# A macaron transformer block in float32: a separate buffer for the softmax sums, one for the attention's transposed tokens, and another order of blocks

## The chip, the core and the metric

The kernel runs on one core of a Trainium2 chip. The metric is the time of one execution on the device in microseconds (us). Each kernel is run several times and the median is compared. The profile is of one further execution.

The engines are called PE (TensorE, matrix products), DVE (VectorE), ACT (ScalarE), POOL (GpSimd) and SP (SyncE, which here only issues DMAs). "PEld" is the loading of a matmul's stationary operand.

## The reference

Eight sequences of 512 tokens with 512 features each go through a half feed-forward network, an attention and another half feed-forward network. Everything is float32.

```python
x = x + 0.5 * ffn(layernorm(x))      # the first half
x = x + attention(layernorm(x))
x = x + 0.5 * ffn(layernorm(x))      # the second half

# ffn: width 2048; of every four neighbours only the two largest are kept
h = silu(x @ w_gate) * (x @ w_up)
h = keep_two_of_four(abs(h)) * h
y = h @ w_down

# attention: 16 heads of 32, 4 key/value heads, rotary positions
scores = einsum('bhqd,bhkd->bhqk', rope(q), rope(k)) / 32 ** 0.5
out = einsum('bhqk,bhkd->bhqd', softmax(scores), v) @ W_o
```

## The kernel before

**Two kinds of work.** The feed-forward work is done in 16 *blocks*, one for each sequence b and each half: (b, 0) is the half before the attention, (b, 1) the one after. A block is a generator (`ffn`) that emits matmuls in *groups*. Its gate and up products (`woven`) are arranged in seven products of quarter matrices instead of eight (a Strassen-like scheme): each `product` is four matmuls of 128x128 by 256 columns, and is called with a PSUM bank named x, v or z. Its down products (y, `products`) are eight such matmuls each. A block has `WIDTH` = 42 groups, and a product of gate and up counts half a group.

Everything else runs *beside* the blocks as *sides*: the layernorm of the next block (`layernorm_t`) and the attention of a sequence (`attention`). A side is a generator too. Between two groups of the block in hand the main loop may let a side take one step, which emits a few instructions. So TensorE's order, a single queue, is: product, product, a step of attention, product, and so on. The work of a side fits where the waits of its operands have passed while TensorE worked on products.

**What decides when a side steps.** The builder keeps its own clock of three engines (`at["pe"]`, `at["dve"]`, `at["act"]`), which it moves on as it emits instructions (`takes`, `multiplied`). Each side has a first and a last group between which its steps are paced, with a weight for each step (`WEIGHTS`). A side steps when its turn has come (`due`) and when what it yielded as *ready* lies before TensorE's time on that clock. If it is `LATE` = 3 groups overdue, it steps regardless. VectorE's work is held in three queues (`urgent`, `put_off`, `for_later`, through `soon` and `later`), from which `fill` takes what fits beside TensorE; `ensure` emits what is asked for at once. All of this only fixes the order of instructions. On the chip, semaphores decide when they run.

**The attention of one sequence.** After its layernorm and the projections of k, q and v, it goes through four quarters of heads c = 0 to 3 (four heads at a time on 32-row tiles of TensorE), and in each through four row tiles t = 0 to 3:

- `scores(c + 1, t)`: four matmuls into sc, four reductions on DVE for the row maxima nm. The maxima are split into three bf16 pieces z (`in_pieces`), transposed by TensorE (tr) and copied by ACT into mT (`pieces_by_row`).
- `exponentials(c, t)`: the transposed scores st, with the maxima subtracted by four small matmuls, then one exponential on ACT from st into p, four heads by 512 at once.
- `weighted`: four matmuls from p into the output ops.
- `summed`: DVE adds the previous p onto this one, in place: p(t) += p(t-1), four adds for each t > 0. As the add changes p(t), it comes after the matmuls `weighted` have read p(t). The buffers for p are two (`p_slots`), used in turn.
- `divided`: after t = 3, four matmuls with ones sum p over rows into den; ACT takes its reciprocal by Ln and Exp (two changes of the function table); DVE multiplies ops by it into qT. It is emitted right behind the next quarter's first st.

There is one PSUM slot of four banks for sc and st, one bank for ops, and three banks for all else (`Bank`).

The attention's own layernormed, transposed tokens xT are in the pool `xtp` with two buffers, which the feed-forward blocks' xT share; the list `in_xT` counts who holds one, and a layernorm's transposes wait until one is free.

**Order of the blocks.** (0,0), (1,0), (2,0), (0,1), (3,0), (1,1), (4,0), (2,1), (5,0), (3,1), (6,0), (4,1), (7,0), (5,1), (6,1), (7,1). An attention begins at the earliest 16 groups after the end of its first half, and must be done 13 groups before its second half; they follow each other. By the formulas in the code they get 55, 59, 72, 72, 65, 58.8, 69.1 and 55 groups, with 7 to 19 groups without an attention in four places.

Of the kernel before, what the change touches and what calls it, by code (L numbers as in the profile page):

```python
# [11 lines left out]
FP = mybir.dt.float32  # L12
# [14 lines left out]
def macaron_block(  # L27
# [59 lines left out]

    Q11, Q12, Q22, Q21, S1, S2, S3, S4 = range(8)
    gu_sums = [dram.tile([P, 4, 2, ND // 2, P], FP, name=f"gu_{i}") for i in range(2 * NCH)]
    blocks = [(0, 0), (1, 0)]  # L90
    for b in range(2, B):
        blocks += [(b, 0), (b - 2, 1)]
    blocks += [(B - 2, 1), (B - 1, 1)]
    coming = deque()
    for block in blocks:
        for i in range(2 * NCH):
# [61 lines left out]
    class Later:  # L158
# [8 lines left out]
        def fits(self, slack):  # L167
            return max(at["dve"], self.ready) + self.us <= at["pe"] + slack

    def later(us, does, ready=None, queue=put_off):  # L170
        queue.append(Later(us, does, pe_heard() if ready is None else ready, queue))
        return queue[-1]
# [42 lines left out]
    class Bank:  # L215
        def __init__(self, shape, name, dtype=FP):
            self.slot = min(banks, key=lambda slot: max(slot[2], when(slot[1]), at["pe"]))
            banks.remove(self.slot)
            takes("pe", 0.0, max(self.slot[2], ensure(self.slot[1])) + TOLD)
            self.slot[1:] = [], 0.0  # L220
            self.tile = ps_mm.tile(shape, dtype, tag=f"mm{self.slot[0]}", name=name)

# [39 lines left out]
    def by_scalar():  # L262

        return at["act"] - BEHIND
# [3 lines left out]
    def layernorm_t(got, tag, src=None, xb=None):  # L268
# [33 lines left out]

        def turn(t):
            if t == 0:
                assert len(in_xT) < 2
                in_xT.append(got)
                got["xT"] = xtp.tile([P, ND, S], FP, tag="xT", name="xT")
            xT = got["xT"]
            tr = transposed([xn[t][:, c * P : (c + 1) * P] for c in range(ND)])
            nc.scalar.copy(xT[:, :, t * P : (t + 1) * P], tr.tile)  # L310
            tr.free(end=takes("act", 0.6, pe_heard()))
# [11 lines left out]
        if xb is None:  # L323
            there = at["pe"] + 10.0
            yield lambda: there
            found = [soon(0.9, partial(moments, t)) for t in (0, 1)]
            yield now
            found += [soon(0.9, partial(moments, t)) for t in (2, 3)]
            yield partial(when, found[:2])
            ensure(found[:2])  # L330
            scales((0, 1))
            yield partial(when, found)
            ensure(found)
            scales((2, 3))
            yield by_scalar
            for t in range(NT):
                normalise(t)
                end = at["act"]
                yield by_scalar if t < NT - 1 else lambda: max(end, by_scalar()) if len(in_xT) < 2 else None
            for t in range(NT):  # L340
                turn(t)
                yield by_scalar if t < NT - 1 else now
            if tag == "xf":
                sums()
        else:

            function(AF.Sqrt)
            for t in range(NT + 1):
                if t < NT:
                    moments(t)  # L350
                    va = rs[:, 0, t : t + 1]
                    nc.vector.tensor_scalar(va, mv[:, t, 1:2], EPS, None, ALU.add)
                    nc.scalar.activation(va, va, AF.Sqrt)
                if t:
                    i = t - 1
                    nc.vector.reciprocal(rs[:, 1, i : i + 1], rs[:, 0, i : i + 1])
                    nc.vector.tensor_scalar(
                        xn[i], xb[:, i, :], mv[:, i, 0:1], rs[:, 1, i : i + 1], ALU.subtract, ALU.mult
                    )
                    turn(i)  # L360
            function(AF.Silu)
            sums()
# [149 lines left out]
    def ffn(b, final, last):  # L512
# [90 lines left out]
        def woven(h, i, r, last_one):  # L603
# [4 lines left out]

            def product(bank, q, rhs, first, ready=0.0):
                lhs = quarters[(b, final), i, q]  # L610
                takes("pe", 0.0, ready + TOLD)
                for m in range(2):
                    for k in range(2):
                        nc.tensor.matmul(  # L614
# [23 lines left out]
            product(x, Q11, b11, True)  # L638
            end = copied(left, x.tile)
            yield 0.5  # L640
            takes("pe", 0.0, ensure(normed[b, final].pop("made", ())) + TOLD)
            v = Bank([P, 2, HALF], "v")
            product(v, S1, ts[:, 0], True, ensure(gu_made.pop(i, ())))
            at_corner = copied(corner, v.tile)
# [117 lines left out]
    def attention(b):  # L762
# [15 lines left out]
        def projected(dst, col, scale):  # L778
# [13 lines left out]
            ps.free([read])  # L792
            soon(0.65, partial(nc.vector.scalar_tensor_tensor, sw, sw, scale, cs[:, 1, :], ALU.mult, ALU.mult))
            made = soon(0.65, partial(nc.vector.tensor_tensor, dst, dst, sw, ALU.add))
            return [p_slots.used(w_slots.used(made))]

        of_k = projected(kT, D, 1.0)
        yield now
# [14 lines left out]
                )  # L813
        multiplied(3.57)
        fill()
        in_xT.remove(got)
        nc.scalar.copy(v, vps.tile)
        vps.free(end=takes("act", 0.6, pe_heard()))
        wo = wa_slots.tile([P, ND, D + 2 * KV], FP, "wo")
# [3 lines left out]
        def scores(c, t, nm):  # L823

            sc = sc_slots.tile([P, N_KV, S], FP, "sc")
            for kv, rows in enumerate(heads):
                nc.tensor.matmul(  # L827
                    out=sc[:, kv, :], lhsT=qT[rows, c, t * P : (t + 1) * P], rhs=kT[rows, :], start=True, stop=True
                )
# [22 lines left out]
            tr.free(end=takes("act", 0.6, pe_heard()))  # L852
            return mT

        def exponentials(c, t, mT):

            st = sc_slots.tile([P, N_KV, S], FP, "st")
            p = p_slots.tile([P, N_KV, S], FP, "p")
            for kv, rows in enumerate(heads):
                nc.tensor.matmul(  # L860
                    out=st[:, kv, :], lhsT=kT[rows, t * P : (t + 1) * P], rhs=qT[rows, c, :], start=True, stop=False
# [4 lines left out]
            multiplied(1.29, True)  # L866
            function(AF.Exp)
            nc.scalar.activation(p, st, AF.Exp)  # L868
            end = takes("act", 1.88, max(pe_heard(), p_slots.ready + 0.1))
            return p, end  # L870

        def weighted(t, ops, p):

# [3 lines left out]
                )  # L877
            multiplied(1.0, True)

        def summed(p, before):  # L880

            if before is None:
                return []
            for kv in range(N_KV):
                made = later(0.6, partial(nc.vector.tensor_tensor, p[:, kv], p[:, kv], before[:, kv], ALU.add))
            return [p_slots.used(p_slots.used(made), 1)]

        def divided(c, ops, p, sums):

            ensure(sums)  # L890
            den = Bank([P, S], "den")
            for kv, rows in enumerate(heads):
                nc.tensor.matmul(out=den.tile[rows, :], lhsT=ones32, rhs=p[:, kv, :], start=True, stop=True)  # L893
            multiplied(1.0, True)
            rT = w_slots.tile([P, S], FP, "rT")
            function(AF.Ln)
# [16 lines left out]
            yield partial(when, found)  # L913
        pieces = in_pieces(nm)
        yield partial(when, pieces)
        p = before = last = None
        out_of = []
        for c in range(ND):
            ensure(pieces)
            mT = pieces_by_row()  # L920
            turned = at["act"]
            nm = maxima()
            for t in range(NT):


                if t == 1:
                    ops = acc_slots.tile([P, S], FP, "ops")
                if p is not None:
                    weighted((t - 1) % NT, ops, p)
                if c + 1 < ND:  # L930
                    found = scores(c + 1, t, nm)
                if p is not None:
                    sums = summed(p, before)
                    before = p if t else None
                    if t == 0:
                        last = (c - 1, ops, p, sums)
                if c + 1 < ND:
                    yield partial(lambda f, turned: max(when(f), turned), found, turned)
                p, end = exponentials(c, t, mT)
                there = []  # L940
                if t == 0 and last is not None:
                    there = out_of = divided(*last)
                elif t == NT - 1 and c + 1 < ND:
                    there = pieces = in_pieces(nm)
                yield partial(lambda there, end: max(when(there), end), there, end)
        weighted(NT - 1, ops, p)
        last = (c, ops, p, summed(p, before))
        yield partial(when, last[3])
        xts = []
        for t in range(NT):  # L950
            xts.append(xnp.tile([P, D], FP, tag="xa", name="xt"))
            nc.sync.dma_start(out=xts[t], in_=tokens[b][1][t * P : (t + 1) * P, :])
        out_of = divided(*last)
        yield partial(when, out_of)
        ensure(out_of)
        for t, xt in enumerate(xts):
            y = Bank([P, D], "y")
            for k in range(ND):
# [21 lines left out]
    NORM = 5 + 2 * NT  # L980

    WEIGHTS = [0.5] * (NORM + ND + 2) + [0.7] * (NT + 1) + [0.9, 0.9] * NT
    WEIGHTS += ([0.9, 1.5] + [0.9, 0.9] * (NT - 1)) * (ND - 2) + [1.5] + [1.3] * (NT - 1) + [0.9] * 2 + [0.5] * NT
    ATTENTION = len(WEIGHTS)

    def place(b, i):
# [4 lines left out]
    for b, i in blocks[1:]:  # L991
        stage = partial(layernorm_t, normed[b, i], "xf", tokens[b][2 * i])
        sides.append((place(b, i) - 15, place(b, i) - 2, NORM, stage, ("attention", b) if i else None, None))
    before = 0
    for b in range(B):

        left = place(B - 1, 1) - 13 - before
        first = max(before, place(b, 0) + WIDTH + 16)
        if first % WIDTH > 17:
            first += WIDTH - first % WIDTH  # L1000
        last = min(place(b, 1) - 13, max(before + left / (B - b), first + 1.4 * WIDTH))
        assert last - first > ATTENTION * 0.8
        sides.append((first, last, ATTENTION, partial(attention, b), ("attention", b - 1) if b else None, ("attention", b)))
        before = last
    sides.sort(key=lambda s: s[0])

    for _ in layernorm_t(normed[0, 0], "xf", xb=xs[0, 0]):
# [98 lines left out]
```

## Time and profile before

| | before |
|---|---|
| median of 3 runs | 3256.96 us (3256.67 to 3257.97) |
| profiled execution, its own time | 3256.3 us |
| its span, first to last instruction | 3254.5 us |
| TensorE clock granted | 0.998 of full speed |
| DMA queue of all tensors, share of 16 engines' time | 42.6% |
| last matmul ends | 4.0 us before the end of the span |

How to read the profile's rows. A *group* row gives source line, engine, operation, output and inputs by name, shapes, the count, then busy time in us and mean ns of one, then the engine's idle time before them and what ended it. A float32 matmul is recorded as two. The matmuls of the tiled stretches (sc, st, ops, den) run four at a time, so the mean of one says little; busy time divided by the number of groups is the figure to use. A *wait* row gives the waiting engine, tile and line, whom it waited for, and then the total in us, the number of waits and the longest. A *timeline* row gives start and duration in us, engine, line, operation and count, and in brackets the idle time before it. Line 164 is the helper that runs DVE's queued work (L164), so its rows are told apart by the tile.

### The profile page before, as it was taken

What the parts mean: (1) busy time and instruction counts of PE and PEld (TensorE: products, weight loads), DVE (VectorE), ACT (ScalarE), POOL (GpSimd) and SP (SyncE); (2) the same over time, 40 slices, a digit from 0 to 9 for tenths busy, and PEclk for the clock granted to TensorE, in tenths of its full rate; (3) what the DMA queues carried; (4) which work ended last, traced back from release to release, by engine and by line L of the source; (5) the groups of instructions that cost most, each with busy time, mean ns of one, the idle gap of its engine ahead of it and who ended that gap; (6) DMA issues with size and microseconds to landing.
All of it is one profiled execution on the core that took longest, in us unless ns stands there. A gap on an engine that the chain in (4) does not pass through costs nothing.

```text
span 3254.5 us, 43735 instructions
## 1 busy us (share of the span) xinstructions
PE 3207.1 (99%) x15880; PEld 2322.9 (71%) x15880; DVE 2274.8 (70%) x4894; ACT 1194.5 (37%) x1680; POOL 603.3 (19%) x888
## 2 busy tenths in 40 slices
PE   8999999999999999999999999999999999999999
PEld 6886668766776667776776668666776678666786
DVE  6867865677677775876678866687577765787554
ACT  2222452145324441354314532146324542255221
POOL 2422002210220112111221112111120122100220
PEclk9999999999999999999999999999999999999999
DMA  6762335433533434444443345333533446234451
GB/s 229 246 218 96 111 126 174 144 120 107 191 111 123 156 114 161 134 129 140 163 147 122 121 148 195 117 117 111 198 99 117 156 128 209 95 109 139 151 174 46
DMA packets 249285, 463.21 MB, mean 142 GB/s; under 512 B 24432, under 2 KB 64368, under 8 KB 248304
## 3 DMA queue, kind: packets, MB, share of 16 engines
q1 hardware_dynamic: 249072, 460.42, 42.6%
q8 instruction: 127, 2.08, 0.3%
q14 instruction: 86, 0.70, 0.1%
HBM read 421.53 MB, written 38.80 MB: 141 GB/s over the span
## 4 chain that ended last, share of the span: by engine, by line
PE 93%; DVE 3%; DMA 1%; ACT 1%; issue 1%; POOL 0%; SPq 0%; DVEq 0%; ACTq 0%; POOLq 0%
PE x L614 25%; PE y L542 23%; PE v L614 12%; PE z L614 6%; PE proj L782 4%; PE sc L827 4%; PE ops L875 4%; PE st L860 4%; PE y L959 3%; PE den L893 2%; PE tr L252 2%; PE gu L589 1%; DVE p L164 1%; PE vps L807 1%; PE y L572 1%; PE st L865 1%
## 5 line engine op out<-in xcount | busy, mean ns | idle before, releaser
L614 PE MATMUL x<-ts,w 128*128 128x256 f32 x3000 | 721.9, 384 | 9.5 <-DVE corner L628 6.4
L614 PEld LDWEIGHTS x<-ts,w 128*128 128x128 f32 x3000 | 560.9, 191 | 157.6 <-issue 55.0
L542 PE MATMUL y<-wd,h 128*128 128x256 f32 x1984 | 451.3, 382 | 6.4 <-ACT rT L897 2.9
L542 PEld LDWEIGHTS y<-wd,h 128*128 128x128 f32 x1984 | 372.4, 190 | 93.1 <-issue 27.5
L436 POOL TENSOR_TENSOR e<-h 128x512 f32<-128x512 f32 x62 | 99.1, 1598 | 1625.2 <-DVE h L430 1504.5
L868 ACT ACTIVATE p<-st 128x2048 f32<-128x2048 f32 x128 | 239.6, 1872 | 392.6 <-DVE p L164 199.6
L164 DVE TENSOR_REDUCE nm<-sc 128x1 f32<-128x512 f32 x512 | 322.2, 683 | 60.7 <-PE sc L827 58.6
L542 PE MATMUL y<-wd,e 128*128 128x256 f32 x1488 | 336.5, 381 | 1.2 <-DMA wd<-wd 1.2
L555 DVE SCALAR_TENSOR_TENSOR x<-y,x 128x512 f32<-128x512 f32 x372 | 242.3, 685 | 131.8 <-PE y L542 129.9
L542 PEld LDWEIGHTS y<-wd,e 128*128 128x128 f32 x1488 | 280.0, 190 | 58.6 <-issue 16.5
L244 ACT ACT_TABLE_LOAD x224 | 287.4, 1283 | 4.7 <-PEq L1095 0.7
L164 DVE TENSOR_TENSOR p<-p 128x512 f32<-128x512 f32 x384 | 256.4, 724 | 32.3 <-PE ops L875 32.3
L232 ACT COPY row<-x 128x512 f32<-128x512 f32 x194 | 113.5, 585 | 404.8 <-PE x L614 403.9
L663 ACT ACTIVATE h<-x 128x256 f32<-128x256 f32 x125 | 47.5, 380 | 576.2 <-PE x L614 544.1
L614 PE MATMUL x<-xT,w 128*128 128x256 f32 x1000 | 240.8, 384 | 0.0
L614 PE MATMUL z<-xT,w 128*128 128x256 f32 x1000 | 239.4, 382 | 0.0
L614 PE MATMUL v<-xT,w 128*128 128x256 f32 x1000 | 238.9, 382 | 0.2
L614 PE MATMUL v<-ts,w 128*128 128x256 f32 x1000 | 238.4, 381 | 0.4 <-DVE ts L164 0.3
L614 PEld LDWEIGHTS x<-xT,w 128*128 128x128 f32 x1000 | 186.7, 191 | 53.7 <-issue 23.4
L614 PEld LDWEIGHTS z<-xT,w 128*128 128x128 f32 x1000 | 186.4, 190 | 49.4 <-issue 22.8
L614 PEld LDWEIGHTS v<-xT,w 128*128 128x128 f32 x1000 | 187.4, 190 | 46.2 <-issue 10.9
L614 PEld LDWEIGHTS v<-ts,w 128*128 128x128 f32 x1000 | 187.6, 190 | 40.4 <-issue 9.1
(106 smaller groups left out, 4067.7 us busy)
## 6 DMA issues: line engine op xcount, KB each, us to landing
w<-gu SPq DMA_DIRECT2D x472, 256.0 KB, 3.3
w<-in_w_gu SPq DMA_DIRECT2D x394, 256.0 KB, 3.3
wd<-wd SPq DMA_DIRECT2D x155, 512.0 KB, 4.0
wd<-in_w_down SPq DMA_DIRECT2D x124, 256.0 KB, 4.9
x<-x SPq DMA_DIRECT2D x64, 256.0 KB, 2.6
xn<-x SPq DMA_DIRECT2D x64, 256.0 KB, 6.8
x<-in_x SPq DMA_DIRECT2D x32, 256.0 KB, 3.3
gu<-w SPq DMA_DIRECT2D x32, 256.0 KB, 2.6
```

The costliest lines, as they stand in the source:

```text
L164: self.does()
L232: nc.scalar.copy(dst, src)
L244: nc.scalar.activation(dummy[:, 1:2], dummy[:, 0:1], f)
L436: nc.gpsimd.tensor_tensor(sums[:, 2], h11, h12, ALU.add)
L542: nc.tensor.matmul(out=y.tile[:, t, :], lhsT=part[:, t * P : (t + 1) * P], rhs=operands[i][:, n, :], start=(n == 0), stop=(n == 3),)
L555: nc.vector.scalar_tensor_tensor(to, y.tile, 0.5 * sign, to, ALU.mult, ALU.add)
L614: nc.tensor.matmul(out=bank.tile[:, m, :], lhsT=lhs[:, m, k, :], rhs=rhs[:, k, :], start=(first and m == 0 and k == 0), stop=(k == 1), ski ...
L782: nc.tensor.matmul(out=ps.tile, lhsT=wa[:, k, col : col + P], rhs=xT[:, k, :], start=(k == 0), stop=(k == ND - 1))
L827: nc.tensor.matmul(out=sc[:, kv, :], lhsT=qT[rows, c, t * P : (t + 1) * P], rhs=kT[rows, :], start=True, stop=True)
L860: nc.tensor.matmul(out=st[:, kv, :], lhsT=kT[rows, t * P : (t + 1) * P], rhs=qT[rows, c, :], start=True, stop=False)
L868: nc.scalar.activation(p, st, AF.Exp)
L875: nc.tensor.matmul(out=ops[rows, :], lhsT=v[:, t, rows], rhs=p[:, kv, :], start=(t == 0), stop=(t == NT - 1))
```

## The change

1. **Sum of exponentials in a buffer of its own.** In each quarter the exponential at t = 0 goes into `total`, those at t = 1, 2, 3 into `other`, one and the same buffer. DVE adds `other` onto `total` (`added`), from the end of the exponential on. `divided` takes den from `total`, and is emitted after the next scores and before the next st. For the last quarter it is emitted right after the last `weighted`, without a step between.
2. **The attention's transposed tokens** take a slot of `p_slots` instead of a buffer of `xtp`. So rope tables (cs), transposed tokens, `total` and `other` use the two slots in turn. Only the blocks' own xT are counted in `in_xT`.
3. **Order of blocks**: (0,0), (1,0), (2,0), (3,0), (0,1), (4,0), (1,1), (2,1), (5,0), (6,0), (3,1), (7,0), (4,1), (5,1), (6,1), (7,1). Every attention gets the same number of groups, (617 - 58) / 8 = 69.9, one right after the other.
4. **The builder's clock** is told of more waits (`waits`): for the slot of sc and st until its exponential is done, for ops, for p, for the pieces, for the sums. Steps yield more of what they need as their readiness. Two weights of the steps become others (1.5 to 1.2, and two of 0.9 to one of 1.5, as there is one step less).

```diff
-    blocks = [(0, 0), (1, 0)]
-    for b in range(2, B):
-        blocks += [(b, 0), (b - 2, 1)]
-    blocks += [(B - 2, 1), (B - 1, 1)]
+    first_of = {0: 0, 1: 1, 2: 2, 3: 3, 5: 4, 8: 5, 9: 6, 11: 7}
+    second_of = {4: 0, 6: 1, 7: 2, 10: 3, 12: 4, 13: 5, 14: 6, 15: 7}
+    blocks = [(first_of[i], 0) if i in first_of else (second_of[i], 1) for i in range(2 * B)]
...
+    class Done:
+        def __init__(self, end):
+            self.end = end
+    def waits(end):
+        takes("pe", 0.0, end + TOLD)
...
             if t == 0:
-                assert len(in_xT) < 2
-                in_xT.append(got)
-                got["xT"] = xtp.tile([P, ND, S], FP, tag="xT", name="xT")
+                if tag == "xf":
+                    assert len(in_xT) < 2
+                    in_xT.append(got)
+                    got["xT"] = xtp.tile([P, ND, S], FP, tag="xT", name="xT")
+                else:
+                    got["xT"] = p_slots.tile([P, ND, S], FP, "xT")
...
-        def exponentials(c, t, mT):
+        def exponentials(c, t, mT, p, free):
             st = sc_slots.tile([P, N_KV, S], FP, "st")
-            p = p_slots.tile([P, N_KV, S], FP, "p")
+            waits(sc_slots.ready)
...
-            end = takes("act", 1.88, max(pe_heard(), p_slots.ready + 0.1))
-            return p, end
+            end = takes("act", 1.88, max(pe_heard(), free + 0.1))
+            sc_slots.used(Done(end))
+            return end
...
-        def summed(p, before):
-            if before is None:
-                return []
+        def added(p, end):
             for kv in range(N_KV):
-                made = later(0.6, partial(nc.vector.tensor_tensor, p[:, kv], p[:, kv], before[:, kv], ALU.add))
-            return [p_slots.used(p_slots.used(made), 1)]
+                made = later(0.6, partial(nc.vector.tensor_tensor, total[:, kv], total[:, kv], p[:, kv], ALU.add), end + HEARD)
+            return [made]
-        def divided(c, ops, p, sums):
-            ensure(sums)
+        def divided(c, ops, sums):
+            waits(ensure(sums))
...
+        total = p_slots.tile([P, N_KV, S], FP, "total")
+        other = p_slots.tile([P, N_KV, S], FP, "p")
...
                 if c + 1 < ND:
                     found = scores(c + 1, t, nm)
-                if p is not None:
-                    sums = summed(p, before)
-                    before = p if t else None
-                    if t == 0:
-                        last = (c - 1, ops, p, sums)
+                out_of = []
+                if t == 0 and c > 0:
+                    out_of = divided(c - 1, ops, sums)
                 if c + 1 < ND:
-                    yield partial(lambda f, turned: max(when(f), turned), found, turned)
-                p, end = exponentials(c, t, mT)
-                there = []
-                if t == 0 and last is not None:
-                    there = out_of = divided(*last)
-                elif t == NT - 1 and c + 1 < ND:
-                    there = pieces = in_pieces(nm)
-                yield partial(lambda there, end: max(when(there), end), there, end)
+                    yield partial(when, there + found)
+                p = other if t else total
+                end = exponentials(c, t, mT, p, ensure(sums))
+                sums = added(p, end) if t else []
+                if t == NT - 1:
+                    out_of += sums
+                    if c + 1 < ND:
+                        pieces = in_pieces(nm)
+                        out_of += pieces
+                yield partial(when, [Done(end)] + out_of)
+        waits(end)
         weighted(NT - 1, ops, p)
-        last = (c, ops, p, summed(p, before))
-        yield partial(when, last[3])
+        out_of = divided(c, ops, sums)
...
-    before = 0
-    for b in range(B):
-        left = place(B - 1, 1) - 13 - before
-        first = max(before, place(b, 0) + WIDTH + 16)
-        if first % WIDTH > 17:
-            first += WIDTH - first % WIDTH
-        last = min(place(b, 1) - 13, max(before + left / (B - b), first + 1.4 * WIDTH))
+    bounds = [WIDTH + 16 + b * (place(B - 1, 1) - 13 - WIDTH - 16) / B for b in range(B + 1)]
+    for b, (first, last) in enumerate(zip(bounds, bounds[1:])):
         sides.append((first, last, ATTENTION, partial(attention, b), ("attention", b - 1) if b else None, ("attention", b)))
-        before = last
```

More of the change, by code (lines that the diff above doesn't have):

```diff
@@ L89, in macaron_block @@
     gu_sums = [dram.tile([P, 4, 2, ND // 2, P], FP, name=f"gu_{i}") for i in range(2 * NCH)]
-    blocks = [(0, 0), (1, 0)]
-    for b in range(2, B):
-        blocks += [(b, 0), (b - 2, 1)]
-    blocks += [(B - 2, 1), (B - 1, 1)]
+    first_of = {0: 0, 1: 1, 2: 2, 3: 3, 5: 4, 8: 5, 9: 6, 11: 7}
+    second_of = {4: 0, 6: 1, 7: 2, 10: 3, 12: 4, 13: 5, 14: 6, 15: 7}
+    assert B == 8
+    blocks = [(first_of[i], 0) if i in first_of else (second_of[i], 1) for i in range(2 * B)]
     coming = deque()
@@ L218, in __init__ @@
             banks.remove(self.slot)
-            takes("pe", 0.0, max(self.slot[2], ensure(self.slot[1])) + TOLD)
+            waits(max(self.slot[2], ensure(self.slot[1])))
             self.slot[1:] = [], 0.0
@@ L338, in layernorm_t @@
                 end = at["act"]
-                yield by_scalar if t < NT - 1 else lambda: max(end, by_scalar()) if len(in_xT) < 2 else None
+                yield by_scalar if t < NT - 1 else (
+                    lambda: max(end, by_scalar()) if tag == "xa" or len(in_xT) < 2 else None
+                )
             for t in range(NT):
@@ L610, in product @@
                 lhs = quarters[(b, final), i, q]
-                takes("pe", 0.0, ready + TOLD)
+                waits(ready)
                 for m in range(2):
@@ L640, in woven @@
             yield 0.5
-            takes("pe", 0.0, ensure(normed[b, final].pop("made", ())) + TOLD)
+            waits(ensure(normed[b, final].pop("made", ())))
             v = Bank([P, 2, HALF], "v")
@@ L794, in projected @@
             made = soon(0.65, partial(nc.vector.tensor_tensor, dst, dst, sw, ALU.add))
-            return [p_slots.used(w_slots.used(made))]
+            return [p_slots.used(w_slots.used(made), 1)]
         of_k = projected(kT, D, 1.0)
@@ L815, in attention @@
         fill()
-        in_xT.remove(got)
         nc.scalar.copy(v, vps.tile)
@@ L853, in pieces_by_row @@
             return mT
-        def exponentials(c, t, mT):
+        def exponentials(c, t, mT, p, free):
             st = sc_slots.tile([P, N_KV, S], FP, "st")
-            p = p_slots.tile([P, N_KV, S], FP, "p")
+            waits(sc_slots.ready)
             for kv, rows in enumerate(heads):
@@ L878, in weighted @@
             multiplied(1.0, True)
-        def summed(p, before):
-            if before is None:
-                return []
+        def added(p, end):
             for kv in range(N_KV):
-                made = later(0.6, partial(nc.vector.tensor_tensor, p[:, kv], p[:, kv], before[:, kv], ALU.add))
-            return [p_slots.used(p_slots.used(made), 1)]
-        def divided(c, ops, p, sums):
-            ensure(sums)
+                made = later(0.6, partial(nc.vector.tensor_tensor, total[:, kv], total[:, kv], p[:, kv], ALU.add), end + HEARD)
+            return [made]
+        def divided(c, ops, sums):
+            waits(ensure(sums))
             den = Bank([P, S], "den")
             for kv, rows in enumerate(heads):
-                nc.tensor.matmul(out=den.tile[rows, :], lhsT=ones32, rhs=p[:, kv, :], start=True, stop=True)
+                nc.tensor.matmul(out=den.tile[rows, :], lhsT=ones32, rhs=total[:, kv, :], start=True, stop=True)
             multiplied(1.0, True)
@@ L915, in attention @@
         yield partial(when, pieces)
-        p = before = last = None
-        out_of = []
+        total = p_slots.tile([P, N_KV, S], FP, "total")
+        other = p_slots.tile([P, N_KV, S], FP, "p")
+        p, sums = None, []
         for c in range(ND):
-            ensure(pieces)
+            waits(ensure(pieces))
             mT = pieces_by_row()
-            turned = at["act"]
+            there = [Done(at["act"])]
             nm = maxima()
             for t in range(NT):
-                if t == 1:
-                    ops = acc_slots.tile([P, S], FP, "ops")
                 if p is not None:
+                    if t == 1:
+                        ops = acc_slots.tile([P, S], FP, "ops")
+                        waits(acc_slots.ready)
+                    waits(end)
                     weighted((t - 1) % NT, ops, p)
@@ L931, in attention @@
                     found = scores(c + 1, t, nm)
-                if p is not None:
-                    sums = summed(p, before)
-                    before = p if t else None
-                    if t == 0:
-                        last = (c - 1, ops, p, sums)
-                if c + 1 < ND:
-                    yield partial(lambda f, turned: max(when(f), turned), found, turned)
-                p, end = exponentials(c, t, mT)
-                there = []
-                if t == 0 and last is not None:
-                    there = out_of = divided(*last)
-                elif t == NT - 1 and c + 1 < ND:
-                    there = pieces = in_pieces(nm)
-                yield partial(lambda there, end: max(when(there), end), there, end)
+                out_of = []
+                if t == 0 and c > 0:
+                    out_of = divided(c - 1, ops, sums)
+                if c + 1 < ND:
+                    yield partial(when, there + found)
[8 more added lines that the diff above has]
+                yield partial(when, [Done(end)] + out_of)
+        waits(end)
         weighted(NT - 1, ops, p)
-        last = (c, ops, p, summed(p, before))
-        yield partial(when, last[3])
+        out_of = divided(c, ops, sums)
         xts = []
@@ L952, in attention @@
             nc.sync.dma_start(out=xts[t], in_=tokens[b][1][t * P : (t + 1) * P, :])
-        out_of = divided(*last)
         yield partial(when, out_of)
-        ensure(out_of)
+        waits(ensure(out_of))
         for t, xt in enumerate(xts):
@@ L982, in macaron_block @@
     WEIGHTS = [0.5] * (NORM + ND + 2) + [0.7] * (NT + 1) + [0.9, 0.9] * NT
-    WEIGHTS += ([0.9, 1.5] + [0.9, 0.9] * (NT - 1)) * (ND - 2) + [1.5] + [1.3] * (NT - 1) + [0.9] * 2 + [0.5] * NT
+    WEIGHTS += ([0.9, 1.2] + [0.9, 0.9] * (NT - 1)) * (ND - 2) + [1.5] + [1.3] * (NT - 1) + [1.5] + [0.5] * NT
     ATTENTION = len(WEIGHTS)
@@ L993, in macaron_block @@
         sides.append((place(b, i) - 15, place(b, i) - 2, NORM, stage, ("attention", b) if i else None, None))
-    before = 0
-    for b in range(B):
-        left = place(B - 1, 1) - 13 - before
-        first = max(before, place(b, 0) + WIDTH + 16)
-        if first % WIDTH > 17:
-            first += WIDTH - first % WIDTH
-        last = min(place(b, 1) - 13, max(before + left / (B - b), first + 1.4 * WIDTH))
-        assert last - first > ATTENTION * 0.8
+    bounds = [WIDTH + 16 + b * (place(B - 1, 1) - 13 - WIDTH - 16) / B for b in range(B + 1)]
+    for b, (first, last) in enumerate(zip(bounds, bounds[1:])):
+        assert place(b, 0) + WIDTH + 16 <= first and last <= place(b, 1) - 13
         sides.append((first, last, ATTENTION, partial(attention, b), ("attention", b - 1) if b else None, ("attention", b)))
-        before = last
     sides.sort(key=lambda s: s[0])
```

## The prediction

> **What bounds the kernel now.** I read the profile page first (engine totals), then the groups of the TensorE instructions, then who TensorE waited for, then the timeline around the worst places. The page:
>
> ```profile
> span 3254.5 us, 43735 instructions
> PE 3207.1 (99%) x15880; PEld 2322.9 (71%) x15880; DVE 2274.8 (70%) x4894; ACT 1194.5 (37%) x1680; POOL 603.3 (19%) x888
> ```
>
> TensorE sets the end: 99% busy, nothing else above 71%. The change adds and removes no matmul, so all it can win is time in which TensorE stands still, plus whatever stands still inside "busy". The first is small. Who TensorE waited for:
>
> ```profile
> PE tr L252 <- DVE xn L357: 7.4, 3, 6.4
> PE x L614 <- DVE corner L628: 6.4, 2, 6.1
> PE sc L827 <- DVE nm L164: 4.1, 4, 1.4
> PE tr L252 <- DVE z L843: 3.6, 2, 1.8
> PE x L614 <- ACT row L232: 3.2, 1, 3.2
> PE ops L875 <- ACT p L868: 3.1, 4, 2.2
> PE y L542 <- ACT rT L897: 2.9, 1, 2.9
> PE ops L875 <- DVE qT L164: 2.8, 2, 1.4
> PE den L893 <- DVE p L164: 1.6, 4, 0.6
> PE st L860 <- DVE nm L164: 1.6, 3, 0.8
> ```
>
> All of TensorE's idle time is 3254.5 - 3207.1 = 47.4 us, 4.0 of it after the last matmul; 43.4 are left. Of these 8.1 is the first layernorm and first matmuls (to 12.5 us) and 10.1 the opening block (68 to 120 us): the instruction order of all engines is the same in both kernels until the first attention's projections, so 18.2 us stay. 3.2 (x on ACT row, at 3055 us) is the last block's layernorm. That leaves 22 us in the eight attentions: sc, z, p, rT, qT, st and den above and a few of 0.3 us.
>
> The second part hides in a busy row. The three groups below are TensorE on 32-row or 32-column tiles; den and ops are four matmuls each (8 records), of one size:
>
> ```profile
> L875 PE MATMUL ops<-p,v 128*32 128x512 f32 x1024 | 136.4, 605 | 6.0 <-ACT p L868 3.1 <-DVE qT L164 2.8
> L893 PE MATMUL den<-p,ones 128*32 128x512 f32 x256 | 56.5, 604 | 2.1 <-DVE p L164 1.6 <-PE st L865 0.3
> ```
>
> ops: 136.4 / 128 groups = 1.07 us. den: 56.5 / 32 = 1.77 us, for the same work. So 0.70 x 32 = 22.4 us of den's "busy" time is TensorE held between its four matmuls. The timeline shows by what:
>
> ```profile
> 2263.22 1.14 PE L860 MATMUL st<-qT,kT 32*128 32x512 f32 x8
> 2263.31 5.17 DVE L164 TENSOR_TENSOR p<-p 128x512 f32<-128x512 f32 x4 [1.90 <-PE ops L875]
> 2264.59 1.05 PE L893 MATMUL den<-p,ones 128*32 128x512 f32 x2
> 2266.26 1.04 PE L893 MATMUL den<-p,ones 128*32 128x512 f32 x2 [0.63 <-DVE p L164]
> 2267.93 1.65 PE L893 MATMUL den<-p,ones 128*32 128x512 f32 x4 [0.63 <-DVE p L164]
> ```
>
> The adds p += before may start only when ops has read p, den stands right behind st, and each den matmul waits for its own add. (Here GpSimd ran beside them and four adds took 5.17; elsewhere they take 2.50.)
>
> As a check on the whole I laid all matmuls of the order end to end at their steady spacing in the trace (product of four 1.73 us, y of eight 3.46, proj and y<-wo 3.43, ops, sc and den 1.05, st 0.95 + 0.31, 0.1 for each change of tiling): 3179.5. Adding 43.4, 22.4 and the 4.0 us after the last matmul gives 3249.3 of the 3254.5 us span; 5 us are unexplained.
>
> **The change, part by part.**
>
> *Sum in its own buffer.* As many adds (384), as many exponentials, 32 of them now into total. What moves is when an add may start: at the end of its exponential, not after ops has read p, and the last sum is asked for one step earlier, with the step held back until the planner has the sums done. From the order: between the end of st and the start of den there are 0.0 us of other matmuls in 24 of 32 cases before; after, never less than 6.9, 28 of 32 at 8.6 or more. What must fit in: 0.1 to hear, the exponential with its table, four adds at 2.50.
>
> Here a rule speaks against the change. The Trainium skill, "ScalarE: Activation LUTs", section "What ACT_TABLE_LOAD costs", puts a change of function at 1283 ns plus a drain of about 1380, 2.66 us. The trace:
>
> ```profile
> 1155.13 1.28 ACT L244 ACT_TABLE_LOAD   x1
> 1156.43 0.20 ACT L244 ACTIVATE dummy<-dummy 128x1 f32<-128x1 f32 x1
> 1156.54 0.58 ACT L897 ACTIVATE rT<-den 128x512 f32<-128x512 f32 x1
> ```
>
> From load to the next function 1.41 us. With the row an exponential is there 0.1 + 1.41 + 1.88 = 3.4 us after st; by the page 4.64. In the changed order 24 of the 128 ops stand only 3.7 us behind their st: by the row they fit, by the page each loses 0.94, 23 us in all, and the forecast would be 3241. But before has 38 at 3.7 and two at 1.9, which by the page would lose 41 us, and ops waited for ACT 3.1. I take the row. Den then needs 3.4 + 2.5 = 5.9 of its 6.9: the 22.4 us go, except where GpSimd doubles the adds (+2.6). GpSimd's 310 long operations (1.27 to 1.71 us each) cover some 450 of 3254 us, 15%, so about 5 of 32; with 1 to 4 us to spare, that leaves 4 us.
>
> The cost of this part: p at t = 1, 2, 3 is one buffer, so each of these exponentials waits for the adds of the one before. On ACT, copies of row and corner and the silus queue behind it, and TensorE's products wait for these. Cover: the next st stands at least 4.7 + 1.05 + 3.0 = 8.7 us behind the last where there are scores between, against 3.4 + 2.5 = 5.9. In the last quarter of heads (no scores) five stand 4.7 + 0.97 behind: 0.2 us late, no cost. Before, ACT already waited for these adds, 199.6 us in 55 cases, at nearly no cost to TensorE.
>
> *den beside ops and sc, the last one too.* The tiled stretches fall from 272 to 264 (the last den stood alone). A change costs 0.09 us on entering and 0.10 on leaving by the spacing of starts: 8 x 0.2 = 1.6 us won; the laid-out order gives 3177.9 against 3179.5, the same. Eight table loads fewer (224 to 216) lie beside TensorE: nothing.
>
> *Waits told to the planner; weights of the steps.* No instruction is added. What they alter is the distance from a request to its use, which I read off the order. Scores behind scores: least 1.9 us before (4 cases), 3.7 after; a reduction of four takes 2.48 plus 0.14 to start, so the stalls of 1.38 and 0.68 at 638 and 2095 us go. Transposed pieces to st: least 1.1, now 2.2. ops behind st: 1.9, now 3.7. st to scores: 3.0, now 4.7. One gets worse: scores to st, least 3.7 before, now 3.0 in five cases (but 26 instead of 56 at 3.7): 3.0 against 2.6, free unless DVE is behind.
>
> *Order of blocks.* Before, attentions take 55 to 72 groups, with holes between; the four of 55 to 59 (from 210, 558, 2014 and 2726 us) hold 16 of the 22 us, the fourth attention (72 groups, from 1233 us) 0.25. After, all eight take 69.9, without holes. DVE's load is hardly the cause: it is busy 223.45 of 305 us (73%) in the first attention and 260.12 of 360 (72%) in the fourth. What counts is the pace of the steps. DMA: the same transfers; the queues' share is 43% and attention's weights followed directly on an attention at 874, 1233 and 2332 us without a stall.
>
> *Transposed tokens in a p slot.* The next block's layernorm no longer waits for the attention's v product; in exchange ACT's first copy into xT waits for the last ops of the attention before, and the rope tables' DMA on SP (ahead of the next gate weights) for its last den. Both are over ten products old by then (four y<-wo lie between): nothing. If that cover went, 16 quarters of weights are ahead, about 28 us of products.
>
> Attention gaps of 22: I keep 1.5 for reductions and 1.5 for ops. Sum: 22 + 22.4 - 7 + 1.6 = 39.0 won. Profiled time 3256.3 (span 3254.5, 1.8 around it) becomes 3217.3; the runs' median 3256.96 stands 0.7 above, so **3218**.
>
> **The rivals.**
> - *den waits as before* (the change doesn't do what it says): adds are put off on DVE and reached only when den asks. For: DVE is 70% busy and adds are the lowest but one in its queue. Against: the step is withheld until they are made. Keeps 22.4 of stall, less the 4 I left anyway: 3218 + 18.4 = 3236.
> - *Everything goes*, the 3.2 at 3055 too (the last attention ends 8.6 us earlier in the order): 3218 - 7 - 3.2 = 3208; with the unexplained 5 us, 3203.
> - *Slower: the one p buffer.* Exponentials chain through DVE's adds, in 3 x 4 x 8 = 96 rounds. It decides from (44.4 + 1.6) / 96 = 0.48 us of TensorE per round; at 0.7 the time is 3257 - 46 + 67 = 3278. For: ACT's 199.6 us of waiting. Against: 8.7 us between rounds for 5.9.
> - *Nothing either way*: new stalls at the new block borders eat the gain, 3257.
>
> **How the numbers follow.** Chances: forecast 0.66, den as before 0.14, everything goes 0.10, nothing 0.04, slower 0.06. So faster 0.90, same 0.04, slower 0.06 (0.2%, 6.5 us, is about what can be told from no change). The range runs from 3204 (all gone and the unexplained too) to 3240 (den as before and 4 us of new stalls, or the page's table price).
>
> **What would show it.** den at 1.07 to 1.2 us a group, about 38 us busy; no "sc on DVE nm" of 1.4 us; TensorE's idle time 25 us instead of 43.4, the opening's 18.2 unchanged; attentions of about 345 us each. Wrong it would be if ops waits for ACT p by tens of us, or den stays near 56 us busy.

## The result, and the profile after

| | before | after |
|---|---|---|
| median of the runs | 3257.02 us (3255.5 to 3257.97, 6 runs) | 3233.73 us (3230.99 to 3234.68, 6 runs) |
| ratio, 95% interval | | 0.9927 (0.9914 to 0.994) |
| profiled execution, its span | 3254.5 us | 3228.9 us |
| TensorE idle before its last matmul | 43.4 us | 42.6 us |
| den, busy for 32 groups | 56.5 us | 33.8 us |

The changed kernel is 0.73% faster: 23.3 us by the medians, 25.6 by the spans. The forecast was 39. TensorE's idle time is nearly the same, and yet it is made of other waits.

The page of the changed kernel:

```profile
span 3228.9 us, 43667 instructions
PE 3182.6 (99%) x15880; PEld 2323.7 (72%) x15880; DVE 2298.6 (71%) x4880; ACT 1191.8 (37%) x1678; POOL 609.3 (19%) x888
```

TensorE's busy time fell by 24.5 us for the same 15880 records. The groups of TensorE, by shape (busy us, mean ns, then idle time before them), show where:

```profile
L892 PE MATMUL ops<-p,v 128*32 128x512 f32 x768 | 102.3, 605 | 0.0
L892 PE MATMUL ops<-total,v 128*32 128x512 f32 x256 | 34.1, 605 | 0.0
L908 PE MATMUL den<-total,ones 128*32 128x512 f32 x256 | 33.8, 599 | 0.0
```

den now takes 33.8 / 32 = 1.06 us a group, as much as ops; it had taken 1.77. So 22.7 us of waiting between den's matmuls are gone, and ops no longer waits for an exponential or for its slot (it had waited 6.0 us).

Who TensorE waited for, after:

```profile
PE y L558 <- DMA wd<-wd: 10.6, 4, 4.6
PE tr L263 <- DVE xn L373: 7.4, 3, 6.4
PE st L876 <- DVE nm L165: 6.7, 4, 1.9
PE x L630 <- DVE corner L644: 6.3, 1, 6.3
PE v L630 <- ACT xT L324: 2.4, 2, 1.5
PE x L630 <- ACT xT L324: 1.8, 2, 0.9
PE tr L263 <- ACT xT L324: 1.5, 2, 0.7
```

sc for nm, the transposes for z, ops for p and for qT, y for rT, den for p: of the waits that made up the attentions' 22 us before, all but one are off this list. The one is st for the maxima nm, which grew from 1.6 us to 6.7 (in four). Beside it stands y for the down weights wd (9.2 of the 10.6 in two waits of 4.6, at 918 and 1969 us; the rest is in the opening block and was there before). The attentions' idle time is 24.6 us instead of the 3 that were forecast.

**The waits for down weights.** SyncE's queue at the first of the two places:

```profile
903.12 0.32 SPq L117 DMA_DIRECT2D w<-gu  x1
903.50 0.42 SPq L782 DMA_DIRECT2D wqkv<-in_w_k  x1
903.97 0.50 SPq L782 DMA_DIRECT2D wqkv<-in_w_q  x1
904.51 0.51 SPq L782 DMA_DIRECT2D wqkv<-in_w_v  x1
905.14 0.55 SPq L786 DMA_DIRECT2D cs<-in_rope  x1
905.73 3.42 SPq L287 DMA_DIRECT2D xn<-x  x4
909.25 2.88 SPq L519 DMA_DIRECT2D wd<-wd  x2
```

An attention begins: eight loads (wqkv, cs and xn) with 1.5 MB of weights, 0.5 MB of rope tables and 1 MB of tokens are issued in one step, and the next down weights stand behind them. TensorE's side of it:

```profile
902.93 3.62 PE L558 MATMUL y<-wd,h 128*128 128x256 f32 x16
906.38 7.07 PE L558 MATMUL y<-wd,e 128*128 128x256 f32 x32
918.04 2.47 PE L558 MATMUL y<-wd,h 128*128 128x256 f32 x5 [4.58 <-DMA wd<-wd]
```

Three products with the loaded weights are done by 913.4, and the fourth set isn't there. A buffer for it came free at 906.4, when the first of the three had read its own. SyncE issued the load at 909.25, behind the attention's, and it landed 8.7 us later, at 918.0 (the next one took 7.3; the median over the kernel is 3.9). The windows around the wait (columns: length, busy time of PE, PEld, DVE, ACT and POOL, each with its number of records, then the granted clock, the DMA engines' busy share, GB/s):

```profile
906.00:913.00 7.00, 7.00 (x34) 6.18 (x33) 6.12 (x17) 3.16 (x4) 1.98 (x8) 1.00 1.01 347
914.60:918.00 3.40, 0.00 (x0) 0.00 (x0) 2.03 (x6) 0.00 (x0) 0.00 (x0) 1.00 0.87 343
918.00:921.40 3.40, 3.36 (x8) 2.77 (x9) 0.00 (x0) 0.00 (x0) 0.00 (x0) 0.50 0.02 7
921.40:924.80 3.40, 3.40 (x17) 2.99 (x17) 1.32 (x3) 0.00 (x0) 0.00 (x0) 0.99 0.00 0
```

The DMA engines are full (1.01) while TensorE runs out of weights. And the wait costs more than its 4.58 us: in the 3.4 us after it the clock is 0.50, and 8 matmul records run where 17 run in the next 3.4 us. That is another 1.7 us for each of the two, inside "busy": y from h is busy 455.1 us after, 451.3 before.

**The waits for maxima.** The timeline before the first of the four, at 690 us:

```profile
679.84 6.13 DVE L165 TENSOR_TENSOR total<-total,p 128x512 f32<-128x512 f32 x4
680.36 1.71 POOL L455 TENSOR_TENSOR e<-h 128x512 f32<-128x512 f32 x1
683.58 1.14 PE L843 MATMUL sc<-kT,qT 32*128 32x512 f32 x8
687.09 1.87 DVE L165 TENSOR_REDUCE nm<-sc 128x1 f32<-128x512 f32 x3
690.22 1.14 PE L876 MATMUL st<-qT,kT 32*128 32x512 f32 x8 [1.85 <-DVE nm L165]
```

Four adds into total take 6.13 us instead of about 2.5, because GpSimd's sums of hidden values run beside them. The reductions of the scores stand behind the adds in DVE's order and begin 2.4 us after the scores are done, and st waits.

### The profile page after: what moved, and what is told of

Read it like the earlier page. It is cut to its first block, busy times and chain, and to the rows that moved or that the text cites. A ratio compares the mean times of both kernels' runs of the same rounds, so it can differ in the third digit from the quotient of the medians.

```text
span 3228.9 us, 43667 instructions
## 1 busy us (share of the span) xinstructions
PE 3182.6 (99%) x15880; PEld 2323.7 (72%) x15880; DVE 2298.6 (71%) x4880; ACT 1191.8 (37%) x1678; POOL 609.3 (19%) x888
## 4 chain that ended last, share of the span: by engine, by line
PE 95%; DVE 2%; DMA 1%; ACT 1%; issue 0%; POOL 0%; SPq 0%; DVEq 0%; ACTq 0%; POOLq 0%
PE x L630 27%; PE y L558 22%; PE v L630 13%; PE z L630 7%; PE proj L798 4%; PE st L876 4%; PE sc L843 4%; PE ops L892 4%; PE y L977 3%; PE tr L263 1%; PE gu L605 1%; PE den L908 1%; PE vps L823 1%; PE st L881 1%; PE y L588 1%; DMA wd<-wd 1%
## 5 line engine op out<-in xcount | busy, mean ns | idle before, releaser
L558 PE MATMUL y<-wd,h 128*128 128x256 f32 x1984 | 455.1, 384 | 12.8 <-DMA wd<-wd 9.5
L452 POOL TENSOR_TENSOR e<-h 128x512 f32<-128x512 f32 x62 | 92.2, 1487 | 1565.5 <-DVE h L446 1346.7
L165 DVE TENSOR_TENSOR total<-total,p 128x512 f32<-128x512 f32 x384 | 282.5, 775 | 45.6 <-ACT p L884 45.6
L884 ACT ACTIVATE p<-st 128x2048 f32<-128x2048 f32 x96 | 179.8, 1873 | 335.4 <-PE st L881 238.9
L243 ACT COPY row<-x 128x512 f32<-128x512 f32 x205 | 120.0, 585 | 357.9 <-PE x L630 357.1
```

The costliest lines, as they stand in the source:

```text
L165: self.does()
L243: nc.scalar.copy(dst, src)
L558: nc.tensor.matmul(out=y.tile[:, t, :], lhsT=part[:, t * P : (t + 1) * P], rhs=operands[i][:, n, :], start=(n == 0), stop=(n == 3),)
```

## The experiments

There were two theories of what the forecast had missed.

- *Places*: two of the eight attentions, the third and the sixth, begin at group 29.75 and 29.4 of a block (197.75 - 4 x 42, 407.4 - 9 x 42), among the down products. The formula that the change took out moved every start that lay past group 17 of its block to the next one.
- *VectorE*: the adds now run where GpSimd holds them up, and DVE's lateness is behind all of it.

Spans below are those of the profiled executions, ratios are to the kernel before.

**The order and places of before, all else changed.**

```diff
-    first_of = {0: 0, 1: 1, 2: 2, 3: 3, 5: 4, 8: 5, 9: 6, 11: 7}
...
-    bounds = [WIDTH + 16 + b * (place(B - 1, 1) - 13 - WIDTH - 16) / B for b in range(B + 1)]
+    blocks = [(0, 0), (1, 0)]
...
+        first = max(before, place(b, 0) + WIDTH + 16)
+        if first % WIDTH > 17:
+            first += WIDTH - first % WIDTH
```

> The changed kernel with the order of blocks and the places of the attentions of before. Theory (the sum buffer wins by den, and the new places cost 13 us because two attentions start at group 29 of a block, among the down products, where their first loads hold up the down weights): den at 34 us busy, no wait of y for wd over 1 us outside the opening block, about 3221 us. Rival (the even places of the attentions win the time): most of the gain is gone, 3245 us or more.

Measured: 3225.88 us, 5 above the expected, ratio 0.9904 (0.9889 to 0.9919), span 3221.2; den 33.7 us. Who TensorE waited for:

```profile
PE y L557 <- DVE h L445: 6.5, 5, 2.5
PE tr L262 <- DVE z L858: 3.6, 2, 1.8
PE sc L842 <- DVE nm L164: 3.4, 3, 1.4
PE y L557 <- DMA wd<-wd: 0.8, 2, 0.4
```

The rival falls: without the new order and places the whole gain is there, and 7.7 us more by the spans (7.9 by the medians; the two intervals just overlap). No y waits long for wd. What this kernel waits for instead is on the first three lines. y waits for hidden values from DVE, 2.5 us at 704 and again at 2149 us; and attentions of 55 to 59 groups still ask for scores 1.9 us after the last ones. This kernel has all parts of the change but the order and the places, so that the gain is the sum buffer's is read from den, not from the time.

**The new order and places alone, on the kernel before.**

```diff
+    first_of = {0: 0, 1: 1, 2: 2, 3: 3, 5: 4, 8: 5, 9: 6, 11: 7}
...
+    bounds = [WIDTH + 16 + b * (place(B - 1, 1) - 13 - WIDTH - 16) / B for b in range(B + 1)]
```

> The kernel before with the new order of blocks and the new places of the attentions alone. Theory: den stays at 56 us busy, the two waits for wd of about 4.6 us appear, the old gaps of the attentions (22 us) shrink to about 9: 3255 us, no difference that can be told. Rival (the even places win): 3240 us or less.

Measured: 3250.26 us, ratio 0.998 (0.9972 to 0.9987), span 3246.4. Better than expected by 5 us, and better than no difference: the interval lies below 1. Den is 6 us shorter (first line; 56.5 before), as its adds take 707 ns in the mean instead of 724; that they met GpSimd less often in this order is likely, but not shown. The attentions' other gaps shrank to 12 us, not to 9. The two waits for wd came as expected (the second line includes 1.2 of the opening block):

```profile
L894 PE MATMUL den<-p,ones 128*32 128x512 f32 x256 | 50.5, 605 | 0.1
PE y L543 <- DMA wd<-wd: 10.0, 4, 4.6
```

So the two waits belong to the places, not to the sum buffer.

**Two starts moved.**

```diff
     bounds = [WIDTH + 16 + b * (place(B - 1, 1) - 13 - WIDTH - 16) / B for b in range(B + 1)]
+    bounds[2], bounds[5] = 210.0, 420.0
```

> The changed kernel with two of eight starts moved: the third attention begins at group 210 instead of 197.75 and the sixth at 420 instead of 407.4, so that none begins later than group 17 of a block; their neighbours become 82 and 58 groups long. Theory: the two waits for wd (4.6 us each) and the 2.0 us of small waits behind each go, 13.2 us in all, and the two attentions of 58 groups cost up to 4 back: 3221 to 3225 us. Rival (the missing time is VectorE's, held by GpSimd): 3232 us or more.

Measured: 3216.5 us, ratio 0.9876 (0.9861 to 0.9891), span 3214.7, 14.2 less than after.

```profile
PE sc L843 <- DVE nm L165: 4.1, 4, 1.4
PE tr L263 <- DVE z L859: 1.8, 1, 1.8
PE y L558 <- DMA wd<-wd: 0.4, 1, 0.4
```

The waits for wd are gone, in a kernel whose adds still meet GpSimd's sums (749 ns in the mean, against 775 after). The two attentions of 58 groups pay on the upper two lines, at 1029 to 1046 and 2074 to 2078 us. The time is 4.5 us below the expected range, for two reasons not foreseen: the half clock behind each wait went too, and with the steps elsewhere no st waited for nm.

**A fourth buffer for down weights.**

```diff
-    wdp = ctx.enter_context(tc.tile_pool(name="wdp", bufs=3))
+    wdp = ctx.enter_context(tc.tile_pool(name="wdp", bufs=4))
...
-            for _ in range(3):
+            for _ in range(4):
                 load()
```

> The changed kernel with four buffers for down weights instead of three, loaded four products ahead; all engines but SP keep their order of instructions. Theory: the wait for wd at 918 and 1969 us falls from 4.6 us to under 1.5 each, nothing else moves: 3225 to 3228 us. Rival (the loads of an attention fill the queues so long that one buffer more doesn't help): the waits stay above 3 us, 3232 us or more.

Measured: 3222.66 us, 2.3 below the expected range, ratio 0.9895 (0.988 to 0.991), span 3221.7, 7.2 less than after. The two waits of 4.6 us are 0.9 and 0.8. Only SP's queue differs in order, so the wait was for the weights' landing and for nothing else in that place. How much of it was the later issue and how much the full DMA engines, no run separates. st still waits 6.7 us. The half clock went at these two places, but came up at two of st's waits (693 and 2160 us), where it hadn't been in the run after; so it gave nothing on balance.

**GpSimd's sums cut short.** e is zero outside 8 of 256 columns in this kernel and h is combined in 8 columns only, so a part of the down products' operands is left out.

```diff
-                    nc.gpsimd.tensor_tensor(sums[:, 2], h11, h12, ALU.add)
+                    short(sums[:, 2], h11, h12, ALU.add)
...
+    def short(out, x, y, op):
+        nc.gpsimd.tensor_tensor(out[:, :, :8], x[:, :, :8], y[:, :, :8], op)
```

> The changed kernel with GpSimd's five sums of the hidden values cut from 256 columns to 8, so part of the down products' operands is left out (e is zero there, h is not combined). Order and operands of all other engines are the same. Theory (three of the four waits of st for the maxima come from adds into total that ran beside GpSimd's sums at two to three times their length): mean of the adds falls from 775 to about 685 ns, st's wait for nm from 6.7 to about 1.0 us, 3225 to 3228 us. Rival (VectorE is simply behind there): adds shorter, but st still waits 4 us or more.

Measured: 3221.06 us, ratio 0.9886 (0.9868 to 0.9904), span 3218.6, 10.3 less than after. The adds into total, first after, then here (count, then min/median/max ns):

```profile
L165 DVE TENSOR_TENSOR total<-total,p x384: 658/685/1809, 333.4 to 2965.1; 128x512 f32<-128x512 f32 x192
```

```profile
L171 DVE TENSOR_TENSOR total<-total,p x384: 659/684/708, 331.3 to 2954.5; 128x512 f32<-128x512 f32 x192
```

The median stays, the long ones are gone (mean 775 to 685 ns), and no st waits for nm any more, not even the fourth, of 1.02 us, which the expectation had left standing. The time is below the expected range; 3.1 of the 10.3 us lie in the opening block, whose idle time varies by more than that over the other runs (15.3 to 19.7 us before 125 us), so they are not put down to the sums. The two waits for wd stay at 4.7 and 4.6:

```profile
PE y L564 <- DMA wd<-wd: 9.5, 3, 4.7
```

So there are two causes, each of which goes without the other: cutting GpSimd's sums takes st's waits and leaves y's, the fourth buffer takes y's and leaves st's. (Moving the two starts took both.)

**The attention's tokens back in the blocks' pool.**

```diff
-                else:
-                    got["xT"] = p_slots.tile([P, ND, S], FP, "xT")
+                in_xT.append(got)
+                got["xT"] = xtp.tile([P, ND, S], FP, tag="xT", name="xT")
```

> The changed kernel with the attention's transposed tokens back in the pool of the blocks' xT, counted there. Theory: this part of the change moves nothing, 3231 to 3237 us, the waits for wd stay. Rival (the blocks' layernorms are held up by it): over 3240 us.

Measured: 3232.29 us, ratio 0.9923 (0.9904 to 0.9941). The waits for wd stay (10.9 us in four). This part of the change moves no time that can be told.

**Both remedies.**

```diff
+    bounds[2], bounds[5] = 210.0, 420.0
...
-    wdp = ctx.enter_context(tc.tile_pool(name="wdp", bufs=3))
+    wdp = ctx.enter_context(tc.tile_pool(name="wdp", bufs=4))
```

> The changed kernel with the two starts moved and four buffers for down weights. If both act on the same wait, nothing adds up: 3216 us as with the starts moved alone, less at most 1.5 us for the waits for wd in the opening block. If the buffers win something else too: 3210 us or less.

Measured: 3215.53 us, ratio 0.9869 (0.9854 to 0.9884), span 3213.7. The two don't add up: they act on the same wait. By the medians the kernel with the two starts moved beats the changed one by 17 us, the one with both by 18.

**The waits told to the builder's clock** have no run: with the new ones taken out, the program has the same instructions in the same order on all five engines. This part of the change does nothing here. The weights of the steps and what the steps yield as readiness were not tried alone.

## Why the prediction was right or wrong

The direction and the range held; the gain was 23 instead of 39. That the range held is partly luck: its upper end was drawn for den waiting as before or for the page's table price, and neither came. What came were waits that the sum had at nothing.

- *Sum in its own buffer*: right, and to the size: 22.4 us of waiting in den were to go, and 22.7 went. The 4 I left for GpSimd at den weren't needed: den had 6.9 us or more of other work before it.
- *Price of a table*: the size of the row, 1.41 us, was right; its place in the sum was wrong, and luck kept that from mattering. The prediction put the load behind st. But the load comes with the dummy activation, which needs nothing of st. Of the 24 ops that stand 3.7 us behind their st, 8 have a load just before their exponential, and it began 0.65 to 7.7 us before st ended. With the 2.66 us that the Trainium skill ("ScalarE: Activation LUTs", "What ACT_TABLE_LOAD costs") gives for a switch to another set of tables, one of the 24 would have been late, by an estimated 0.3 us, and not 23 us in all. So that ops waits for no exponential does not decide between the two prices, and neither did ops' few waits before; the row itself does.
- *Table of waits of before*: right. The old waits went (and the 3.2 at 3055), the opening's 18.2 stayed (18.0). Only st's waits for nm did not go but grew.
- *Waits told to the clock, weights of the steps*: the distances I read were those of the program, but I gave them to the wrong part. Taking the new waits out changes no instruction. The distance of scores behind scores is the pace's: with the new weights and readiness it is 1.9 us again in attentions of 55 to 59 groups (with the order of before, and with the starts moved). What makes the others stays open.
- *Scores to st*: the forecast said "3.0 against 2.6, free unless DVE is behind", and kept 1.5 us for reductions. Measured: 6.7. DVE was behind, by GpSimd, and not in the cases at 3.0: the four stood 3.7 to 5.4 us behind their scores. I had put the price of doubled adds to den alone. The adds' first victim is what stands behind them on their own engine.
- *The step that failed* is in "Order of blocks": "attention's weights followed directly on an attention at 874, 1233 and 2332 us without a stall". True of these three, but they start at groups 17, 5 and 16.8 of their block, ahead of its last down products. The formula being removed saw to that, and I never worked out the new starts' groups within a block, though it is one division. The cover I named, 16 quarters or 28 us, is that of the gate weights. Down weights have three buffers, and one comes free only when its product is done, so two products, 7.1 us (906.4 to 913.4), cover a load. This load had 2.8 us of it left uncovered by its place behind the attention's eight loads (issue at 909.25), and then took 8.7 us with the DMA engines full.

The sum with what was measured, by spans: 39.0 forecast; less 21.6 (24.6 us of gaps in the attentions instead of 3: 9.2 for wd, 4.0 in small waits of the layernorm within 35 us behind the two of wd, 6.7 for nm, 4.7 others); less 1.7 for the half clock (3.4 after, against 1.7 before, at 657 us); plus the 4 kept for den and the 3.2 at 3055. That makes 22.9, against 25.6; 2.7 us are unexplained. The runs' median stands 2.7 us above the profiled one, not 0.7 as assumed: the profiled execution was the fastest of six.

## What to carry to other kernels

Look into "busy" for waiting: where a matmul group of the same size is busy longer than its neighbour, something holds it between its matmuls, and no list of waits shows that. When a schedule is redone, ask of every rule that it drops what it had kept apart: here one line kept an attention's eight loads out of the stretch whose weights are least deep. And a burst of loads is hidden by the shallowest prefetch that stands behind it in the queue, not by the deepest.

## What the runs showed of the hardware

- An idle stretch of 4.6 us on TensorE was followed by 3.4 us at half its clock (0.50), so its price was 6.3. The Trainium skill, "TensorE: Matmul & The Clock Gate", "Part 1: The HAM clock gate", states that the clock falls to half after an idle window of about 3.4 us. The length of the slow stretch agrees. But in these runs it also came after shorter idle times: before, at 657 us, behind a wait of 1.81 us, with TensorE busy 5.19 of the 7 us ahead; with the fourth buffer at 693 us, behind 1.86 us and 5.14 of 7. It did not come before at 2112 us, behind the same wait of 1.81 and 5.19 of 7, nor after at 690 us, behind 1.85. So after such a wait executions of one kernel may differ by 1.7 us. The granted clock of the six runs of the changed kernel goes with their time, from 0.998 in the fastest to 0.996 in the three slowest; that this is all of their spread of 3.7 us is not shown.
- An add of DVE with both operands in SBUF takes up to 1.81 us beside GpSimd's sums of some 1.7, and never over 0.71 with these sums cut to 8 columns. The Trainium skill, "SBUF — State Buffer", section "Who interferes with whom", states that a DVE instruction with two inputs in SBUF contends with a GpSimd instruction that reads SBUF, through ports which one of them holds alone. The way from there to TensorE was, in this case, through the reductions queued behind the adds.
